# A convolution and a Mamba layer on one core: decays made two units ahead, and TensorE in order of emission in the last image

## The chip, the cores and the metric

The kernel runs on one core of a Trainium2 chip, as one program and one launch. A core has a TensorE (PE: matrix multiplications and transposes, into PSUM), a VectorE (DVE), a ScalarE (ACT), a GpSimd (POOL) and a SyncE (SP, which issues most of the transfers here). Each engine works through its own list of instructions in order, and waits at semaphores for the others. The metric is the time of one execution in microseconds (us) on the device. Times are medians of several executions; the profile is one more execution, recorded by the hardware profiler.

## The reference

The input x holds four images of 128 x 128 positions and 128 channels, float32. Two layers follow each other, each adding to x:

```python
x = x + _L0_conv_ref(_gn(x), ...)   # deformable 3x3 convolution, two groups of 64 channels
x = x + _L1_conv_ref(_gn(x), ...)   # two Mamba blocks along each row
```

`_gn` normalises groups of four channels over a whole image. The first layer predicts nine offsets for each position and group by a 3x3 convolution, samples the image bilinearly there, and multiplies with a depthwise and a pointwise weight. The second layer treats each row of an image as a sequence of 128 steps. One of its two Mamba blocks is:

```python
u, res = split(h @ in_w)                       # 128 -> 2 x 256
u = silu(conv1d(u) + cb)                       # causal, 4 taps, per channel
dt, Bm, Cm = split(u @ xw)                     # 8, 16, 16
delta = softplus(dt @ dtw + dtb)
h_t = exp(delta_t * A) * h_(t-1) + delta_t * u_t * Bm_t     # 256 channels x 16 states
y_t = sum over the states of h_t * Cm_t, plus u_t * Dp
out = (y * silu(res)) @ ow
```

So each row needs a scan over 128 steps for 256 x 16 channel and state pairs: a decay exp(delta A), an input delta u B, the scan, the product with C and the sum over the states.

## The kernel before

**Stages.** The normalisation of the second layer needs the whole image after the first, so image b of the second layer runs beside image b+1 of the first. The program has: the first layer of image 0 alone (to about 3.3 ms); three mixed stages (second layer of image 0, 1, 2 beside the first layer of image 1, 2, 3); and the second layer of the last image alone (from about 20.12 ms).

**First layer.** For each four rows and each of nine taps POOL gathers the corner pixels with indirect DMAs (`gather`, L370), DVE or ACT multiplies them with the bilinear weights (`sample`, `gw`, L398 on DVE and L393 on ACT, 16 instructions of 64 columns there), PE transposes and sums them (`p`, L137), ACT copies them out (`s`, L416, L417, L413), and PE multiplies with the weights (`acc`, L427). These names turn up in the mixed stages beside the second layer's.

**Second layer.** A job is one block of four rows (512 columns) and one of the two Mamba blocks; an image has 64 jobs, in pairs of blocks, so that a job's successor does not depend on it. `pre` makes what the scan needs, in pieces between which the job before it goes on: the projection with the convolution's four taps (`pu`, L554), SiLU (`u`, L564), the gate (`pr`, L569; `g`, L574), B, C and dt (`pdb`, L578; `dbl`, L581; B and C go to DRAM as `bcd`), and softplus. Softplus is made of Abs and Relu of `pdt` (L600, L603, L604), Exp (L605), 1 + e (L606), Ln (L607) and one step that takes back the rounding of 1 + e. In the first three images PE adds up the four terms by multiplying with the identity (`pdl`, L621, copied out at L622); in the last image DVE does it in three operations (L611 to L613). Then `du` = delta u (L624).

`main` runs the scan in eight units of two states each. For one unit:
- ACT makes the decays into a buffer `da` [128, 2 channel halves, 2 states, 4 rows, 128 steps]: a zero for the first step of each row (L655), and four Exp (L660). There are three such buffers (`das`, `NDA = 3`).
- In the first three images B and C come from DRAM spread over the partitions (`bc0`, `bc1`, issued on SP); DVE multiplies `du` with B (`hs`, L694), scans 2048 columns at once (L700), and multiplies with C (L703). In the last image POOL and ACT multiply the transposed `du` (`duts`, made in `turn_du`) with B (`xs`, L679 for the first state on POOL, L677 for the second on ACT), PE transposes it back (`px`, L684, 16 transposes into four PSUM banks, of which there are four), DVE scans four times 512 columns (L686) and multiplies with C (L689).
- PE transposes the result and adds it to `y` in PSUM (L137, `y`, 16 instructions a unit). There is one `y`, which the job starts with u D (L639).

After the eighth unit comes the job's tail: `g` = y gate on DVE (L710), its transposes (`pyg`, L715), copies (`yg`, L716), the output projection (`pout`, L720, or L727 and L729 with the residual), and a copy out (L722, L733).

**What sets the order.** The Python program emits all instructions in one sequence: `layer1` goes through the jobs, advances `pre` of the next job by one piece after each unit (`next(nxt, None)`), and the loop at the end puts steps of the first layer between the units. The compiler of the framework then schedules: on each engine it takes, by its own model of the costs, the earliest emitted instruction that is ready. The list that results is fixed; on the chip an engine waits at its next instruction, whatever stands behind it. A tile pool with a given number of buffers lets a new tile in when an old one is released. With `manual_schedule` an engine's instructions keep the order of emission.

Of the kernel before, what the change touches and what calls it, by code (L numbers as in the profile page):

```python
# [10 lines left out]
F32 = mybir.dt.float32  # L11
I32 = mybir.dt.int32
AF = mybir.ActivationFunctionType
ALU = mybir.AluOpType
# [3 lines left out]
P = 128  # L18
# [4 lines left out]
SR = 4  # L23
TB = SR * P
# [3 lines left out]
NC = 2  # L28
NS = 16
NQ = 2  # L30
# [34 lines left out]
def block_kernel(ctx: ExitStack, tc: tile.TileContext, a: dict, out: bass.AP):  # L65
# [69 lines left out]
    def add_transposed(o, v, start, stop):  # L135

        nc.tensor.matmul(o, v, ident, is_transpose=True, start=start, stop=stop, skip_group_check=True)  # L137
# [342 lines left out]
    NDA = 3  # L480
# [32 lines left out]
    def in_last(blk):  # L513

        return blk * SR // H == B - 1
# [19 lines left out]
    def pre(st, l):  # L535
# [68 lines left out]
            nc.scalar.activation(de[:, c], pdt, AF.Relu)  # L604
        nc.scalar.activation(e, e, AF.Exp, scale=-1.0)  # L605
        nc.scalar.activation(w1, e, AF.Identity, bias=1.0)  # L606
        nc.scalar.activation(du, w1, AF.Ln)  # L607
        if in_last(blk):
            nc.scalar.activation(w1, w1, AF.Identity, bias=-1.0)
            yield  # L610
            nc.vector.tensor_tensor(e, w1, e, ALU.subtract)  # L611
            nc.vector.tensor_tensor(de, de, e, ALU.subtract)
            nc.vector.tensor_tensor(de, de, du, ALU.add)  # L613
        else:
            nc.scalar.activation(w1, w1, AF.Identity, scale=-1.0, bias=1.0)
            yield
            yield
            for c in range(NC):
                pdl = now["ps1"].tile([P, TB], F32, tag="t", name=f"pdl_{nm}_{c}")
                for k, v in enumerate((e, w1, du, de)):  # L620
                    nc.tensor.matmul(pdl, ident, v[:, c], start=(k == 0), stop=(k == 3))  # L621
                nc.scalar.copy(de[:, c], pdl)  # L622
# [5 lines left out]
            yield  # L628
            turn_du(st, nm)

    def main(st, l):
# [11 lines left out]
        if in_last(blk) and "dut" not in st:  # L643
            turn_du(st, nm)
        for q in range(NS // NQ):
            bc = []
            for w in range(in_last(blk), 2):
                t = lm[0].tile([P, NQ, TB], F32, tag=f"bc{w}", name=f"bc{w}_{nm}_{q}", bufs=2)
                n0 = w * NS + q * NQ
                nc.sync.dma_start(t, st["bcd"][n0 : n0 + NQ, :].partition_broadcast(P))  # L650
                bc.append(t)
            da = das[n_da[0] % NDA]
            n_da[0] += 1

            nc.scalar.copy(da.rearrange("p c n s t -> p (c n s) t")[:, :, 0], zero)  # L655
            for c in range(NC):
                dv = st["delta"][:, c].rearrange("p (s t) -> p s t", s=SR)
                for n in range(NQ):
                    s = q * NQ + n
                    nc.scalar.activation(  # L660
                        da[:, c, n, :, 1:], dv[:, :, 1:], AF.Exp, scale=aneg[:, l, c, s : s + 1]
                    )
            dc = da.rearrange("p c n s t -> p c (n s t)")
            cv = bc[-1].rearrange("p n t -> p (n t)").unsqueeze(1).to_broadcast([P, NC, NQ * TB])
            if in_last(blk):


                for n in range(NQ):
                    s = q * NQ + n

                    xs = lm[0].tile(
                        [P, SR, NC * P], F32, tag="bc0" if n else "gw", name=f"xs_{nm}_{s}", bufs=2
                    )
                    for i in range(SR):
                        bv = st["bt"][:, i, s : s + 1]
                        if n:
                            nc.scalar.activation(xs[:, i], st["dut"][:, i], AF.Copy, scale=bv)  # L677
                        else:
                            nc.gpsimd.tensor_scalar(xs[:, i], st["dut"][:, i], bv, None, ALU.mult)  # L679
                    for c in range(NC):  # L680
                        pool, tag = (now["ps"], "t") if n else (psa, "acc")
                        px = pool.tile([P, SR, P], F32, tag=tag, name=f"px_{nm}_{s}_{c}")
                        for i in range(SR):
                            nc.tensor.transpose(px[:, i, :], xs[:, i, c * P : (c + 1) * P], ident)  # L684
                        dn = da[:, c, n].rearrange("p s t -> p (s t)")
                        nc.vector.tensor_tensor_scan(  # L686
                            dn, dn, px.rearrange("p s t -> p (s t)"), 0.0, ALU.mult, ALU.add
                        )
                nc.vector.tensor_tensor(dc, dc, cv, ALU.mult)  # L689
            else:  # L690
                hs = lm[0].tile([P, NC, NQ, TB], F32, tag="hs", name=f"hs_{nm}_{q}")

                for n in range(NQ):
                    nc.vector.scalar_tensor_tensor(  # L694
                        hs[:, :, n, :], st["du"], one,
                        bc[0][:, n].unsqueeze(1).to_broadcast([P, NC, TB]),
                        op0=ALU.mult, op1=ALU.mult,
                    )
                df = da.rearrange("p c n s t -> p (c n s t)")
                nc.vector.tensor_tensor_scan(  # L700
                    df, df, hs.rearrange("p c n t -> p (c n t)"), 0.0, ALU.mult, ALU.add
                )
                nc.vector.scalar_tensor_tensor(dc, dc, one, cv, op0=ALU.mult, op1=ALU.mult)  # L703
            for c in range(NC):
                for n in range(NQ):
                    for i in range(SR):
                        add_transposed(y[:, i, c], da[:, c, n, i, :], False, q == NS // NQ - 1 and n == NQ - 1)
            yield
        gt = st["g"]
        nc.vector.tensor_tensor(gt, y.rearrange("p s c d -> p s (c d)"), gt, ALU.mult)  # L710
        yg = lm[0].tile([P, NC, TB], F32, tag="yg", name=f"yg_{nm}")
        for c in range(NC):
            pt = now["ps1"].tile([P, SR, P], F32, tag="t", name=f"pyg_{nm}_{c}")
            for i in range(SR):
                nc.tensor.transpose(pt[:, i, :], gt[:, i, c * P : (c + 1) * P], ident)  # L715
            nc.scalar.copy(yg[:, c], pt.rearrange("p s t -> p (s t)"))  # L716
        po = now["ps1"].tile([P, TB], F32, tag="t", name=f"pout_{nm}")
        if l < NL - 1:
            for c in range(NC):
                nc.tensor.matmul(po, ow[:, l, c, :], yg[:, c], start=(c == 0), stop=(c == NC - 1))  # L720
# [136 lines left out]
```

## Time and profile before

| what | value |
|---|---|
| median of 3 executions | 24469.56 us (24467.03 to 24477.43) |
| profiled execution, its own time | 24467.72 us |
| its span in the profile | 24465.9 us, 304806 instructions |
| scans of the mixed stages on DVE (L700) | 1536, 4.42 us each, 3357.9 to 20123.5 us |
| scans of the last image (L686) | 2048, 1.20 us each, 20148.8 to 24448.4 us |
| decays on ACT (L660) | 8192, 0.71 us each |
| DVE busy | 20647.2 us (84% of the span) |
| the profile's granted PE clock, mean | 0.928 |

How to read the profile. An instruction is named by engine, line of the kernel, operation, what it writes and what it reads. A row of a timeline gives its start, its duration, and in brackets the idle time of the engine ahead of it and what ended it; `x16` at the end means 16 instructions one after another. A group's or line's row gives min, median and max of one in ns, and below it in us and times what its engine sat idle for ahead of it. A row of windows gives start and end, its length, then the busy time of PE, PE's weight loads (PEld), DVE, ACT and POOL with the number of instructions, the granted PE clock, the DMA share and GB/s. A row of waits gives who waited, for whom, us in total, times, and the longest. PE's matmul in float32 shows as two instructions.

### The profile page before, as it was taken

The numbers are of one execution on the slowest core, as the hardware profiler recorded it, in microseconds if no ns is written. First come the engines' busy times: TensorE is split into PE (matmuls) and PEld (weight loads), VectorE is DVE, ScalarE is ACT, GpSimd is POOL, SyncE is SP. The second block draws the span as 40 slices with busy tenths as digits, with TensorE's granted clock in tenths as the row PEclk, the third lists the DMA queues.
The fourth block names the chain that finished last, engine by engine and source line by source line (L and its number), as shares of the span: only waits on it lengthen the run. The fifth ranks groups of instructions, "written<-read, shape, count | busy, mean of one in ns | idle before, by whom it ended". The sixth has DMA issues, their size and how long they took to land. (4 is left out here: it accounts for less than half of the span.)

```text
span 24465.9 us, 304806 instructions
## 1 busy us (share of the span) xinstructions
PE 20571.8 (84%) x109348; PEld 12814.4 (52%) x109348; DVE 20647.2 (84%) x12769; ACT 15875.8 (65%) x36074; POOL 18054.1 (74%) x11270
## 2 busy tenths in 40 slices
PE   5777788888888888888888888888988878777777
PEld 3444445555555555555555555555555546666666
DVE  3332369999999999999999999999999998888888
ACT  1111147777777767777777766777777768888887
POOL 4777778888888857888888857888888845555555
PEclk7888889999999999999999999999999989999999
DMA  5554544554545544554555544455545532222221
GB/s 150 155 157 125 149 132 160 162 162 163 163 161 165 162 148 161 162 162 162 162 164 163 163 148 159 163 161 163 164 162 164 162 126 69 70 70 70 69 70 68
DMA packets 1530702, 3470.14 MB, mean 142 GB/s; under 512 B 243283, under 2 KB 717651, under 8 KB 1529052
## 3 DMA queue, kind: packets, MB, share of 16 engines
q1 hardware_dynamic: 1086812, 2242.08, 28.5%
q0 software_dynamic: 442368, 1208.55, 15.5%
q8 instruction: 859, 14.07, 0.2%
q14 instruction: 663, 5.43, 0.1%
HBM read 3299.19 MB, written 150.47 MB: 141 GB/s over the span
## 5 line engine op out<-in xcount | busy, mean ns | idle before, releaser
L370 POOL DMA_INDIRECT gt<-table,idx x9216 | 15702.9, 1704 | 4130.4 <-issue 2793.6
L700 DVE TENSOR_TENSOR_SCAN da<-da,hs 128x2048 f32<-128x2048 f32 x1536 | 6792.7, 4422 | 810.7 <-ACT da L660 708.2
L660 ACT ACTIVATE da<-de,aneg 128x508 f32<-128x508 f32 x8192 | 5450.1, 711 | 1447.6 <-PE y L137 1313.8
L427 PE MATMUL acc<-s,wc 128*64 128x512 f32 (+2 forms) x23520 | 5854.9, 609 | 143.0 <-ACT s L416 136.1
L137 PE MATMUL y<-ident,da 128*128 128x128 f32 x32768 | 4410.3, 291 | 1187.1 <-DVE da L703 911.6
L137 PEld LDWEIGHTS y<-ident,da 128*128 128x128 f32 x32768 | 3936.2, 150 | 2099.3 <-DVE da L703 1028.3
L679 POOL TENSOR_SCALAR xs<-duts,bt 128x256 f32<-128x256 f32 x2048 | 2350.4, 1164 | 2249.6 <-ACT duts L532 1190.4
L694 DVE SCALAR_TENSOR_TENSOR hs<-du,misc,bc 128x1024 f32<-128x1024 f32 x3072 | 3829.4, 1283 | 0.2
L137 PE MATMUL p<-ident,gw 128*128 128x128 f32 x18432 | 2592.6, 293 | 1375.2 <-DVE gw L398 1359.0
L427 PEld LDWEIGHTS acc<-s,wc 128*64 128x64 f32 (+1 forms) x23520 | 1940.7, 141 | 3368.5 <-issue 2999.7
L703 DVE SCALAR_TENSOR_TENSOR da<-da,misc,bc 128x2048 f32<-128x2048 f32 x1536 | 3609.3, 2350 | 39.0
L398 DVE TENSOR_TENSOR gw<-gt,wt 128x1024 f32<-128x1024 f32 x1440 | 1756.1, 1220 | 2219.3 <-DMA gt<-table,idx 2010.2
L393 ACT ACTIVATE gw<-gt,wt 128x64 f32<-128x64 f32 x13824 | 3487.9, 337 | 93.0 <-DMA gt<-table,idx 86.0
L137 PEld LDWEIGHTS p<-ident,gw 128*128 128x128 f32 x18432 | 2247.6, 151 | 1972.1 <-DVE gw L398 1513.7
L686 DVE TENSOR_TENSOR_SCAN da<-da,px 128x512 f32<-128x512 f32 x2048 | 2350.4, 1202 | 506.6 <-PE px L684 506.6
L416 ACT COPY s<-p 128x512 f32<-128x512 f32 x1152 | 671.3, 583 | 2332.7 <-PE p L137 2330.6
L554 PE MATMUL pu<-hp,inc 128*128 128x512 f32 x4096 | 1823.0, 593 | 0.2 <-ACT duts L532 0.2
L684 PE MATMUL px<-ident,xs 128*128 128x128 f32 x8192 | 1210.6, 287 | 542.9 <-DVE da L686 328.2
L684 PEld LDWEIGHTS px<-ident,xs 128*128 128x128 f32 x8192 | 968.5, 147 | 824.1 <-POOL xs L679 331.0
L413 ACT COPY s<-halo 128x256 f32<-128x256 f32 x1116 | 433.4, 401 | 1220.4 <-PE acc L427 1218.4
L689 DVE TENSOR_TENSOR da<-da,bc 128x2048 f32<-128x2048 f32 x512 | 1172.2, 2290 | 6.5
L554 PEld LDWEIGHTS pu<-hp,inc 128*128 128x128 f32 x4096 | 746.9, 189 | 821.1 <-issue 820.4
(148 smaller groups left out, 17815.0 us busy)
## 6 DMA issues: line engine op xcount, KB each, us to landing
bc<-bcd SPq DMA_DIRECT2D x3584, 512.0 KB
gt<-table,idx POOLq DMA_INDIRECT x9216
table<-xg SPq DMA_DIRECT2D x1016, 64.0 KB
xt<-in_x SPq DMA_DIRECT2D x124, 320.0 KB
xr<-in_x SPq DMA_DIRECT2D x128, 256.0 KB
x<-xo SPq DMA_DIRECT2D x128, 256.0 KB
x1t<-x SPq DMA_DIRECT2D x128, 256.0 KB
x1t_o<-x SPq DMA_DIRECT2D x128, 256.0 KB
```

The source lines that it names most:

```text
L137: nc.tensor.matmul(o, v, ident, is_transpose=True, start=start, stop=stop, skip_group_check=True)
L370: nc.gpsimd.indirect_dma_start(out=gt[:, v, r], out_offset=None, in_=flat, in_offset=bass.IndirectOffsetOnAxis(ap=idx[:, ri, o : o + 1], a ...
L393: nc.scalar.activation(gw[:, r, s, v], gts[h][:, v, r, s * CG : (s + 1) * CG], AF.Copy, scale=wt[:, u, r0 + r, s, v : v + 1],)
L427: nc.tensor.matmul(accs[b, j][CG * g : CG * g + CG, q, :], wc[sl, v, e, :], st[p + 4 * g if p < 4 else 8][sl, ky + q.start : ky + q.stop, ...
L554: nc.tensor.matmul(px.rearrange("p (s t) -> p s t", s=SR), inc[:, l, j, c * P : (c + 1) * P], h[:, :, j : j + P], start=(j == 0), stop=(j ...
L660: nc.scalar.activation(da[:, c, n, :, 1:], dv[:, :, 1:], AF.Exp, scale=aneg[:, l, c, s : s + 1])
L679: nc.gpsimd.tensor_scalar(xs[:, i], st["dut"][:, i], bv, None, ALU.mult)
L684: nc.tensor.transpose(px[:, i, :], xs[:, i, c * P : (c + 1) * P], ident)
L686: nc.vector.tensor_tensor_scan(dn, dn, px.rearrange("p s t -> p (s t)"), 0.0, ALU.mult, ALU.add)
L694: nc.vector.scalar_tensor_tensor(hs[:, :, n, :], st["du"], one, bc[0][:, n].unsqueeze(1).to_broadcast([P, NC, TB]), op0=ALU.mult, op1=ALU. ...
L700: nc.vector.tensor_tensor_scan(df, df, hs.rearrange("p c n t -> p (c n t)"), 0.0, ALU.mult, ALU.add)
L703: nc.vector.scalar_tensor_tensor(dc, dc, one, cv, op0=ALU.mult, op1=ALU.mult)
```

## The change

Four things are changed.

1. The decays become a function of their own, `decays`. Two units are made ahead at the start, and then each unit emits the decays of the unit two later, directly after its product with C, ahead of its own transposes. A queue runs over all jobs, so the decays of a job's first two units are emitted in units 6 and 7 of the job before. `delta` is handed over as soon as it is made.
2. What else a unit needs, the broadcasts of B and C and in the last image `xs` and `px`, becomes `head`, and is emitted one unit ahead, before the transposes of `y`; the first unit of a job has its `head` in the last unit of the job before (`after`, which first finishes `pre`). The job's tail is emitted ahead of the step of the first layer, no longer behind it.
3. In the last image PE keeps the order of emission (`manual_schedule`).
4. In the last image softplus is added up by PE as in the others, and the three DVE operations go. In the other images there is one more break between the pieces of `pre`, ahead of Ln.

```diff
         nc.scalar.activation(w1, e, AF.Identity, bias=1.0)
+        if not in_last(blk):
+            yield
         nc.scalar.activation(du, w1, AF.Ln)
-        if in_last(blk):
-            nc.scalar.activation(w1, w1, AF.Identity, bias=-1.0)
+        nc.scalar.activation(w1, w1, AF.Identity, scale=-1.0, bias=1.0)
+        yield
+        if not in_last(blk):
             yield
-            nc.vector.tensor_tensor(e, w1, e, ALU.subtract)
-            nc.vector.tensor_tensor(de, de, e, ALU.subtract)
-            nc.vector.tensor_tensor(de, de, du, ALU.add)
-        else:
...
+        for c in range(NC):
+            pdl = now["ps1"].tile([P, TB], F32, tag="t", name=f"pdl_{nm}_{c}")
+            for k, v in enumerate((e, w1, du, de)):
+                nc.tensor.matmul(pdl, ident, v[:, c], start=(k == 0), stop=(k == 3))
+            nc.scalar.copy(de[:, c], pdl)
+        st["delta"] = de
+        if not in_last(blk):
             yield
         nc.vector.tensor_tensor(du, de, u, ALU.mult)
...
+    def decays(st, l, q):
+        da = das[n_da[0] % NDA]
+        n_da[0] += 1
+        nc.scalar.copy(da.rearrange("p c n s t -> p (c n s) t")[:, :, 0], zero)
...
+                nc.scalar.activation(
+                    da[:, c, n, :, 1:], dv[:, :, 1:], AF.Exp, scale=aneg[:, l, c, s : s + 1]
+                )
+        made.append(da)
+    def head(st, l, q):
...
+        if in_last(blk) and "dut" not in st:
+            turn_du(st, nm)
...
+            nc.sync.dma_start(t, st["bcd"][n0 : n0 + NQ, :].partition_broadcast(P))
...
+                for c in range(NC):
+                    pool, tag = (now["ps"], "t") if n else (psa, "acc")
+                    px = pool.tile([P, SR, P], F32, tag=tag, name=f"px_{nm}_{s}_{c}")
+                    for i in range(SR):
+                        nc.tensor.transpose(px[:, i, :], xs[:, i, c * P : (c + 1) * P], ident)
+                    pxs[n, c] = px
+        return bc, pxs
+    def main(st, l, first, after):
...
+        ahead = first
         for q in range(NS // NQ):
+            bc, pxs = ahead
+            da = made.pop(0)
...
+            last = q == NS // NQ - 1
+            for f in queue[:1]:
+                decays(*queue.pop(0))
+            ahead = after() if last else head(st, l, q + 1)
             for c in range(NC):
                 for n in range(NQ):
                     for i in range(SR):
...
-            yield
+            if not last:
+                yield
...
+    queue = [(st, l, q) for st, l in jobs for q in range(NS // NQ)]
+    made = []
     def layer1():
...
+        for _ in range(NDA - 1):
+            decays(*queue.pop(0))
+        firsts = {0: head(*jobs[0], 0)}
         for i, job in enumerate(jobs):
+            if i and in_last(job[0]["blk"]) and not in_last(jobs[i - 1][0]["blk"]):
+                ctx.enter_context(tc.manual_schedule(engines={mybir.EngineType.PE}))
             nxt = pre(*jobs[i + 1]) if i + 1 < len(jobs) else iter(())
+            def after(i=i, nxt=nxt):
+                for _ in nxt:
+                    pass
+                if i + 1 < len(jobs):
+                    firsts[i + 1] = head(*jobs[i + 1], 0)
-            for _ in main(*job):
+            for _ in main(*job, firsts.pop(i), after):
                 next(nxt, None)
                 yield
-            for _ in nxt:
-                pass
+            yield
```

More of the change, by code (lines that the diff above doesn't have):

```diff
@@ L606, in pre @@
         nc.scalar.activation(w1, e, AF.Identity, bias=1.0)
+        if not in_last(blk):
+            yield
         nc.scalar.activation(du, w1, AF.Ln)
-        if in_last(blk):
-            nc.scalar.activation(w1, w1, AF.Identity, bias=-1.0)
+        nc.scalar.activation(w1, w1, AF.Identity, scale=-1.0, bias=1.0)
+        yield
+        if not in_last(blk):
             yield
-            nc.vector.tensor_tensor(e, w1, e, ALU.subtract)
-            nc.vector.tensor_tensor(de, de, e, ALU.subtract)
-            nc.vector.tensor_tensor(de, de, du, ALU.add)
-        else:
-            nc.scalar.activation(w1, w1, AF.Identity, scale=-1.0, bias=1.0)
-            yield
[L617 to L622, printed above, removed]
+        for c in range(NC):
[5 more added lines that the diff above has]
+        if not in_last(blk):
             yield
@@ L629, in pre @@
             turn_du(st, nm)
-    def main(st, l):
+    def decays(st, l, q):
[3 more added lines that the diff above has]
+        for c in range(NC):
+            dv = st["delta"][:, c].rearrange("p (s t) -> p s t", s=SR)
+            for n in range(NQ):
+                s = q * NQ + n
+                nc.scalar.activation(
[3 more added lines that the diff above has]
+    def head(st, l, q):
+        blk = st["blk"]
+        nm = f"{blk}_{l}"
+        if in_last(blk) and "dut" not in st:
+            turn_du(st, nm)
+        bc = []
+        for w in range(in_last(blk), 2):
+            t = lm[0].tile([P, NQ, TB], F32, tag=f"bc{w}", name=f"bc{w}_{nm}_{q}", bufs=2)
+            n0 = w * NS + q * NQ
+            nc.sync.dma_start(t, st["bcd"][n0 : n0 + NQ, :].partition_broadcast(P))
+            bc.append(t)
+        pxs = {}
+        if in_last(blk):
+            for n in range(NQ):
+                s = q * NQ + n
+                xs = lm[0].tile(
+                    [P, SR, NC * P], F32, tag="bc0" if n else "gw", name=f"xs_{nm}_{s}", bufs=2
+                )
+                for i in range(SR):
+                    bv = st["bt"][:, i, s : s + 1]
+                    if n:
+                        nc.scalar.activation(xs[:, i], st["dut"][:, i], AF.Copy, scale=bv)
+                    else:
+                        nc.gpsimd.tensor_scalar(xs[:, i], st["dut"][:, i], bv, None, ALU.mult)
+                for c in range(NC):
+                    pool, tag = (now["ps"], "t") if n else (psa, "acc")
+                    px = pool.tile([P, SR, P], F32, tag=tag, name=f"px_{nm}_{s}_{c}")
+                    for i in range(SR):
+                        nc.tensor.transpose(px[:, i, :], xs[:, i, c * P : (c + 1) * P], ident)
+                    pxs[n, c] = px
+        return bc, pxs
+    def main(st, l, first, after):
         blk = st["blk"]
@@ L642, in main @@
                 )
-        if in_last(blk) and "dut" not in st:
-            turn_du(st, nm)
+        ahead = first
         for q in range(NS // NQ):
[L646 to L662, printed above, removed]
+            bc, pxs = ahead
+            da = made.pop(0)
             dc = da.rearrange("p c n s t -> p c (n s t)")
@@ L668, in main @@
                 for n in range(NQ):
[L669 to L679, printed above, removed]
                     for c in range(NC):
[L681 to L684, printed above, removed]
                         dn = da[:, c, n].rearrange("p s t -> p (s t)")
                         nc.vector.tensor_tensor_scan(
-                            dn, dn, px.rearrange("p s t -> p (s t)"), 0.0, ALU.mult, ALU.add
+                            dn, dn, pxs[n, c].rearrange("p s t -> p (s t)"), 0.0, ALU.mult, ALU.add
                         )
@@ L706, in main @@
                     for i in range(SR):
-                        add_transposed(y[:, i, c], da[:, c, n, i, :], False, q == NS // NQ - 1 and n == NQ - 1)
-            yield
+                        add_transposed(y[:, i, c], da[:, c, n, i, :], False, last and n == NQ - 1)
+            if not last:
+                yield
         gt = st["g"]
```

## The prediction

> **What bounds the kernel now.** I read the windows by stage first, then what VectorE (DVE) waits for, then the timelines at the waits.
>
> ```profile
> PE 20571.8 (84%) x109348; PEld 12814.4 (52%) x109348; DVE 20647.2 (84%) x12769; ACT 15875.8 (65%) x36074; POOL 18054.1 (74%) x11270
> 3700.00:9150.00 5450.00, 4774.61 (x24640) 2854.55 (x24640) 5109.80 (x2740) 3874.45 (x9388) 4364.02 (x2258) 0.94 0.50 161
> ...
> 20125.00:24460.00 4335.00, 3462.46 (x21631) 2697.95 (x21632) 3810.94 (x2879) 3471.50 (x6213) 2350.45 (x2048) 0.94 0.21 69
> ```
>
> The columns are PE, PEld, DVE, ACT, POOL. In the three mixed stages (second line) DVE is busy 94%, in the last image 88%. So DVE bounds both, and what counts is its idle time.
>
> ```profile
> L700 DVE TENSOR_TENSOR_SCAN da<-da,hs x1536: 4351/4425/4491, 3357.9 to 20123.5; 128x2048 f32<-128x2048 f32 x192
>   ACT da L660: 708.2, 152
> ...
> DVE da L686 <- PE px L684: 506.6, 145, 13.4
> ```
>
> DVE's idle time has two causes. In the mixed stages the scan waits 708.2 us for decays from ScalarE (ACT). In the last image it waits 506.6 us for TensorE's (PE's) transposes. One wait of the first kind:
>
> ```profile
> 7797.29 0.71 ACT L660 ACTIVATE da<-de,aneg 128x508 f32<-128x508 f32 x1
> ...
> 7803.46 1.06 ACT L605 ACTIVATE e<-e 128x1024 f32<-128x1024 f32 x1
> ...
> 7807.26 1.06 ACT L607 ACTIVATE du<-w 128x1024 f32<-128x1024 f32 x1
> ...
> 7810.57 1.28 ACT L660 ACT_TABLE_LOAD   x1
> ...
> 7814.48 0.71 ACT L660 ACTIVATE da<-de,aneg 128x508 f32<-128x508 f32 x1
> 7815.22 4.42 DVE L700 TENSOR_TENSOR_SCAN da<-da,hs 128x2048 f32<-128x2048 f32 x1 [6.02 <-ACT da L660]
> ```
>
> Between one unit's last decay (7797.29) and the next unit's (7814.48) ACT has done the next job's softplus, 16 sampling products and two table loads: 17.2 us, where DVE needs about 10.4 us a unit (jobs start 87.4 us apart there; less 3.7 us of waits, over 8). I numbered the units in their jobs: 682 of the 708 us belong to scans with such a block in front of their last decay.
>
> And the last image, DVE first, then PE:
>
> ```profile
> 21038.38 2.26 DVE L689 TENSOR_TENSOR da<-da,bc 128x2048 f32<-128x2048 f32 x1
> 21047.30 3.44 DVE L686 TENSOR_TENSOR_SCAN da<-da,px 128x512 f32<-128x512 f32 x3 [6.66 <-PE px L684]
> ...
> 21037.98 3.60 PE L554 MATMUL pu<-hp,inc 128*128 128x512 f32 x8
> 21041.42 1.91 PE L137 MATMUL y<-ident,da 128*128 128x128 f32 x16
> 21043.16 3.60 PE L554 MATMUL pu<-hp,inc 128*128 128x512 f32 x8
> 21046.60 1.47 PE L684 MATMUL px<-ident,xs 128*128 128x128 f32 x12
> ```
>
> PE does the next job's projection before the transposes that DVE waits for. Such waits are 530 us in 64 jobs, 8.3 of a job's 67.5 us. The other 59.2 us DVE works.
>
> **The change, part by part.** Where each instruction of the changed kernel stands on its engine is read from the program's lists; durations are from the rows of before.
>
> *Mixed stages, decays two units ahead.* Of ACT's order I counted, in each of some 190 jobs, in front of which unit's last decay the softplus's Ln stands, and summed ACT's work from the last decay before it. Before: unit 4 in 21 jobs (22.1 us of work), unit 5 in 64 (18.0), unit 6 in 104 (15.4). The waits at those units are 186, 308 and 188 us, so 8.9, 4.8 and 1.8 a job: in each case about the block less 13.3 us (22.1 - 8.9, 18.0 - 4.8, 15.4 - 1.8). After: unit 6 in 189 jobs, mean 11.3 us; 34 blocks are near 16 us, the rest 12 or less. By the same rule 34 x 2.7 = 92 us are left, and 590 of 682 go. ACT's total work and the table loads of these stages stay (793 loads before, 775 after). What DVE then runs into: a decay's buffer is free only after PE's transposes of three units earlier (ACT waited 997 us for those between 4000 and 20000), and PE falls behind at each job's start, because y has one buffer (around 7760, unit 0's product ends on DVE at 7759.6 and its transposes start at 7774.37, behind the job before's tail); POOL is busy 80%, and 0.3 us lie between two of its gathers. Softplus moves a unit later, so du stands directly ahead of its first scan, where before a unit lay between. I give 70 us for all this: -520 us. Bounds: 0 (the block, now always at unit 6, costs the time it saved at 4 and 5) and -682.
>
> SP's broadcasts move ahead of the transposes; no scan waited for one, and none is added. The output's tail goes ahead of the image's sampling step: same instructions, nothing on DVE.
>
> *Last image, softplus on PE.* Three DVE operations a job go (L611 to L613, 1.13 us each in a row): -3.4 us. PE gains 16 matmul instructions, 8 pairs at 0.86 us:
>
> ```profile
> 8164.48 1.02 PE L621 MATMUL pdl<-e,ident 128*128 128x512 f32 x2
> ...
> 8170.68 1.02 PE L621 MATMUL pdl<-de,ident 128*128 128x512 f32 x2
> ```
>
> That is 6.9 us; ACT gains two copies (0.48 each) and, by its order, 8 table loads a job instead of 6: 3.5 us on 54.2 of 67.5, hidden by its idle time.
>
> *Last image, PE in order of emission.* The order of a unit q is: px(q+1), y(q), then a piece of the next job. I walked one job, from the end of unit 4 on DVE, with a DVE unit of 6.75 us (4 x 1.13 + 2.2), px 1.85, y 1.8:
> - The projection pieces: the rest of px 1.4, y 1.8, the piece 3.45 and the next first px 0.5 make 7.15 us against DVE's 6.75: it waits 0.4 twice. This replaces the wait of 6.66 shown.
> - After y(5) comes the sum pdl. It needs the last softplus step on ACT. ACT gets pdt 2.8 us after unit 4 ends, needs 8.6 (21063.52 to 21072.1 in the timeline) and now also stands waiting for y(5) with a buffer's first column ahead of Ln: ready at 12.4, when PE, there at 8.65, has waited 2.9 us. pdl ends at 18.5, px(7) is there at 19.1, DVE was ready at 13.5: 5.6 us of waiting. Queued behind pdl are px(7), y(6) and pdu.
> - Then du, pdu and two copies; POOL multiplies xs (0.92 to 1.17 us each, five ahead of the fourth needed) and the next job's first px is there 3.0 us late (from du's end, 21.3 on the walk's clock, to 29.8; DVE was ready at 26.9). y(7) stands behind it on PE.
> - The tail: g, pyg, copies, pout (21030.49 to 21035.06 in the timeline for g's start to pout's end, 4.6 us; about 1 more in the second layer), all of the next y's start (1.9) and px (0.6) now stand in front of the second unit's scans: 4.6 + 0.5 + 1.9 + 0.6 less g's own 1.1 on DVE, 6.4 us.
>
> Waits 0.8 + 5.6 + 3.0 + 6.4 = 15.8 instead of 8.3. A job is 59.2 - 3.4 + 15.8 = 71.6 us, 4.1 more, x 64 = +260 us. Bounds: if ACT and POOL are never late, 2.4 for pdl, 1.8 for POOL (five at 0.92), 5.5 for the tail and 0.4 leave 65.9 us, -100; if each of the three hand-overs through ACT meets one more table load (1.3), +500. I take the walk, whose rows are of this stage.
>
> **Two rules of the Trainium skill.** In the rows a table load takes 1283 ns and the next activation starts 10 ns later (21068.49 and 21069.78). "ScalarE: Activation LUTs", What ACT_TABLE_LOAD costs, gives 2.66 us with a drain, which would make pdl's wait 1.4 us longer, +90 us; no such drain is in these rows, so I leave it out.
> PE is busy 80% of the last image and PEld 62%. "Perfetto Trace Analysis", Identifying the Most-Contended Engine, counts PE's room by LDWEIGHTS: by it 6.9 us more would fit, and the sum would be the second rival's. The walk says otherwise, because of PE's order and not of its load.
>
> **The sum.** -520 + 260 = -260 on the profiled execution's 24467.7 (span 24465.9 and 1.8 around it): 24208. The median shown is 1.9 above it: 24210.
>
> **Rivals.**
> - *Slower.* PE's late y holds ACT at the decays, which now stand ahead of softplus, and what queues behind them (softplus, sampling products, copies) comes as late as before: only 120 of the 590 us go. It speaks for it that PE's y is what ACT waits for most; against it that the waits sit at the softplus blocks. 24467.7 - 120 + 260 = 24608. It decides once less than 260 us go, that is once more than 2.3 of the 3.7 us that a job waits now (708 us in 192 jobs) stay.
> - *Both gain.* The order of emission does what it looks like, px is there before each scan, waits of some 3.5 us a job remain: 59.2 - 3.4 + 3.5 = 59.3, -525 us in the last image: 24467.7 - 520 - 525 = 23420. Against it: the three in-order waits walked above.
> - *No change.* The waits move from units 4 and 5 to unit 6 (104 jobs there waited 1.8 each; 189 x 1.8 = 340 left, 340 saved) and the last image costs 340 too, inside its bounds: 24468.
>
> **How the numbers follow.** Forecast 0.52, own range 23990 to 24420 (main -650 to -350, last +130 to +350); slower 0.23; both gain 0.13; no change 0.12. The range 23850 to 24640 leaves out most of the second rival and the far end of the first. A measurement tells 0.2% (49 us) from no change. Faster: 0.51 + 0.13 + 0.03 = 0.67; same: 0.01 + 0.02 + 0.07 = 0.10; slower 0.23.
>
> **What would show it.** In the profile after: the scan's wait for decays under 150 us and at unit 6 alone (right), or above 450 (first rival); a DVE mixed stage busy 97% and about 170 us shorter; a last image 4.55 to 4.65 ms long, DVE waiting for px at units 1, 7 and 0 of each job, with pdl ahead of px on PE. Wrong if softplus on ACT comes earlier against PE than walked, or if gathers become what DVE waits for.

## The result, and the profile after

The changed kernel takes 24690.4 us (median of 4 runs, 24678.8 to 24706.8) against 24473.5 us of the kernel before on the same chip: a ratio of 1.0088, 95% interval 1.0072 to 1.0104. It is slower by 217 us, where 260 us less were forecast. The profiled execution has a span of 24686.8 us.

First the page's line of busy times of the changed kernel, then two windows, one in the first mixed stage and one over the last image (columns: stretch, its length, busy time of PE, PEld, DVE, ACT and POOL, granted clock, DMA share, GB/s).

```profile
PE 21088.9 (85%) x110372; PEld 13054.0 (53%) x110372; DVE 20500.3 (83%) x12577; ACT 16067.7 (65%) x36312; POOL 17978.0 (73%) x11270
3700.00:8800.00 5100.00, 4586.69 (x23801) 2716.89 (x23800) 4903.09 (x2628) 3726.28 (x9062) 4260.32 (x2191) 0.95 0.51 165
19778.00:24669.00 4891.00, 3992.29 (x22562) 2989.01 (x22563) 3624.76 (x2682) 3678.51 (x6447) 2144.15 (x2037) 0.89 0.18 61
```

In the mixed stage DVE is now busy 96% (4903.09 of 5100) instead of 94%. In the last image it is busy 74% instead of 88%, and the clock that PE was granted there has fallen from 0.94 to 0.89. From DVE's first product with C to its last (L705) the last image takes 4891 us instead of 4296: 595 us more. From the first scan of the mixed stages to the last image's first product it is 3370.9 to 19778.0 instead of 3357.9 to 20153.4: 388 us less. These two make the result; the 13 us by which the first scan starts later are the rest of it, but for a few us.

What DVE's scan in the mixed stages waited for, and then DVE's longest wait in the last image:

```profile
L716 DVE TENSOR_TENSOR_SCAN da<-da,hs x1536: 4352/4425/4493, 3370.9 to 19760.6; 128x2048 f32<-128x2048 f32 x192
  ACT da L639: 199.2, 102
  PE y L137: 28.7, 10
...
DVE da L702 <- PE px L676: 1247.7, 210, 9.7
```

The wait for decays fell from 708.2 to 199.2 us. The wait for px rose from 506.6 to 1247.7 us.

One job of the last image, DVE from unit 6's product on (L705 is the product, L702 the scan, L622 du, L731 the gate), then PE over the same time:

```profile
21361.56 2.29 DVE L705 TENSOR_TENSOR da<-da,bc 128x2048 f32<-128x2048 f32 x1
21371.94 1.22 DVE L702 TENSOR_TENSOR_SCAN da<-da,px 128x512 f32<-128x512 f32 x1 [8.09 <-PE px L676]
21373.08 1.20 DVE L622 TENSOR_TENSOR du<-de,u 128x1024 f32<-128x1024 f32 x1
...
21383.11 4.55 DVE L702 TENSOR_TENSOR_SCAN da<-da,px 128x512 f32<-128x512 f32 x4 [3.16 <-PE px L676]
21387.70 2.29 DVE L705 TENSOR_TENSOR da<-da,bc 128x2048 f32<-128x2048 f32 x1
21389.91 1.22 DVE L731 TENSOR_TENSOR g<-y,g 128x1024 f32<-128x1024 f32 x1
21399.48 4.55 DVE L702 TENSOR_TENSOR_SCAN da<-da,px 128x512 f32<-128x512 f32 x4 [8.36 <-PE px L676]
...
21359.28 1.02 PE L617 MATMUL pdl<-e,ident 128*128 128x512 f32 x2
21363.56 2.08 PE L617 MATMUL pdl<-w,ident 128*128 128x512 f32 x2 [3.25 <-ACT w L610]
21365.42 1.68 PE L617 MATMUL pdl<-du,ident 128*128 128x512 f32 x2
21366.94 1.02 PE L617 MATMUL pdl<-de,ident 128*128 128x512 f32 x2
...
21371.23 1.91 PE L676 MATMUL px<-ident,xs 128*128 128x128 f32 x16
...
21391.18 1.97 PE L736 MATMUL pyg<-ident,g 128*128 128x128 f32 x8 [2.96 <-DVE g L731]
21392.97 3.78 PE L741 MATMUL pout<-yg,w_ow 128*128 128x512 f32 x4
21396.54 2.39 PE L688 MATMUL y<-ddiag,u 128*128 128x128 f32 x16
21398.78 1.91 PE L676 MATMUL px<-ident,xs 128*128 128x128 f32 x16
```

The three waits stand where the prediction put them: behind pdl at unit 7 (8.09), behind POOL's xs at unit 0 of the next job (3.16) and behind the tail at its unit 1 (8.36). Over all jobs they average 8.4, 3.2 and 7.6 us. What was not foreseen is seen in PE's durations: the pair of w behind the wait takes 2.08 us and the same pair without a wait 1.02; pout takes 3.78 us. The windows over this job show why (last but two column: granted clock; the fourth and fifth are cut where the clock changes):

```profile
21362.00:21366.00 4.00, 2.44 (x3) 1.18 (x4) 1.85 (x1) 2.30 (x5) 0.00 (x0) 0.67 0.27 81
21370.00:21374.00 4.00, 4.00 (x30) 3.23 (x29) 2.06 (x2) 3.52 (x6) 0.00 (x0) 1.00 0.00 0
21382.00:21386.00 4.00, 3.58 (x17) 3.40 (x17) 2.89 (x3) 0.00 (x0) 4.00 (x5) 0.50 0.17 64
21387.23:21390.63 3.40, 0.99 (x9) 0.75 (x7) 3.37 (x3) 3.11 (x8) 3.40 (x2) 1.00 0.00 0
21390.64:21397.47 6.83, 6.29 (x17) 4.00 (x18) 0.49 (x1) 2.40 (x5) 0.14 (x1) 0.50 0.20 77
21398.00:21402.00 4.00, 4.00 (x39) 4.00 (x38) 2.52 (x3) 1.22 (x3) 2.02 (x3) 1.00 0.03 6
```

After each wait of about 3 us PE runs at half speed for some us, and in the last of these stretches (clock 0.50 from 21390.64 to 21397.47) it does so while everything on the path behind it (pyg, pout, the next y's start) is waited for. PE's last product ahead of it had ended at 21388.2, so the clock was halved 2.4 us into the wait. "TensorE: Matmul & The Clock Gate" in the Trainium skill, Part 1 (The HAM clock gate), says that PE's clock is halved once PE has idled for a window of about 3.4 us, and is given back after about as long a busy one. The trace agrees on the half (0.50 in two windows, 2.08 against 1.02 us); that the clock fell 2.4 us into a wait of 2.96 us is below the page's figure.

### The profile page after: what moved, and what is told of

The parts are those of the page before. It is cut to its first block, busy times and chain, and to the rows that moved or that the text cites. A ratio compares the mean times of both kernels' runs of the same rounds, so it can differ in the third digit from the quotient of the medians.

```text
span 24686.8 us, 306803 instructions
## 1 busy us (share of the span) xinstructions
PE 21088.9 (85%) x110372; PEld 13054.0 (53%) x110372; DVE 20500.3 (83%) x12577; ACT 16067.7 (65%) x36312; POOL 17978.0 (73%) x11270
## 4 chain that ended last, share of the span: by engine, by line
POOL 24%; PE 24%; DVE 16%; issue 16%; ACT 14%; DMA 5%; SPq 0%; DVEq 0%; POOLq 0%; ACTq 0%
POOL gt L370 23%; DVE da L716 6%; ACT da L639 5%; PE acc L427 5%; DMA gt<-table,idx 4%; PE pdl L617 4%; DVE hs L710 3%; PE pu L554 3%; PE y L137 3%; DVE da L719 3%; PE px L676 2%; POOL xs L671 1%; ACT gw L393 1%; DVE da L702 1%; PE y L688 1%
## 5 line engine op out<-in xcount | busy, mean ns | idle before, releaser
L716 DVE TENSOR_TENSOR_SCAN da<-da,hs 128x2048 f32<-128x2048 f32 x1536 | 6791.7, 4422 | 339.1 <-ACT da L639 199.2
L137 PE MATMUL y<-ident,da 128*128 128x128 f32 x32768 | 4316.5, 284 | 530.7 <-DVE da L719 466.8
L137 PEld LDWEIGHTS y<-ident,da 128*128 128x128 f32 x32768 | 3856.3, 147 | 1239.7 <-DVE da L719 578.0
L671 POOL TENSOR_SCALAR xs<-duts,bt 128x256 f32<-128x256 f32 x2048 | 2156.4, 1072 | 2993.4 <-ACT duts L532 1712.9
L137 PE MATMUL p<-ident,gw 128*128 128x128 f32 x18432 | 2724.8, 291 | 1292.7 <-DVE gw L398 1153.2
L702 DVE TENSOR_TENSOR_SCAN da<-da,px 128x512 f32<-128x512 f32 x2048 | 2336.6, 1201 | 1253.9 <-PE px L676 1247.7
L705 DVE TENSOR_TENSOR da<-da,bc 128x2048 f32<-128x2048 f32 x512 | 1173.5, 2292 | 17.3
L736 PE MATMUL pyg<-ident,g 128*128 128x128 f32 x2048 | 424.6, 375 | 840.5 <-DVE g L731 840.4
```

The lines of the kernel that those rows point to most:

```text
L702: nc.vector.tensor_tensor_scan(dn, dn, pxs[n, c].rearrange("p s t -> p (s t)"), 0.0, ALU.mult, ALU.add)
L716: nc.vector.tensor_tensor_scan(df, df, hs.rearrange("p c n t -> p (c n t)"), 0.0, ALU.mult, ALU.add)
```

## The experiments

The theories were: M, the order of emission on PE makes the last image slow; S, the softplus on PE does; C, PE's slow clock after its waits enlarges what M makes. After the first three runs two more came up: H, the heads and decays ahead cost in the last image; and within H, D (decays) against P (heads). The table has, of each profiled run, the ratio of its time to that of the kernel before measured beside it, and from the last image the stretch from first to last product, the mean job and the granted clock.

| kernel | ratio, 95% | last image, us | job, us | clock |
|---|---|---|---|---|
| before | 1 | 4296 | 67.4 | 0.94 |
| changed | 1.0088 (1.0072 to 1.0104) | 4891 | 76.7 | 0.89 |
| ahead_only | 0.9955 (0.9938 to 0.9971) | 4564 | 71.7 | 0.85 |
| dve_soft | 1.0065 (1.0049 to 1.0082) | 4836 | 75.9 | 0.82 |
| pe_sched | 0.9985 (0.9975 to 0.9994) | 4650 | 73.0 | 0.89 |
| mix_only | 0.9842 (0.9826 to 0.9859) | 4309 | 67.6 | 0.93 |
| mix_dec | 0.9886 (0.9870 to 0.9903) | 4382 | 68.8 | 0.92 |
| mix_head | 0.9941 (0.9924 to 0.9957) | 4527 | 71.1 | 0.86 |
| mix_soft | 0.9903 (0.9887 to 0.9920) | 4426 | 69.5 | 0.95 |
| px_first | 1.0122 (1.0106 to 1.0139) | 4986 | 78.2 | 0.88 |
| tail_late | 1.0040 (1.0026 to 1.0054) | 4779 | 75.1 | 0.89 |
| filler | 1.0045 (1.0028 to 1.0062) | 4809 | 75.4 | 0.92 |
| warm | 1.0068 (1.0051 to 1.0085) | 4840 | 75.9 | 0.96 |
| warm2 | 1.0051 (1.0034 to 1.0068) | 4782 | 75.0 | 0.95 |

Beside mix_dec, mix_head, mix_soft and warm the kernel before itself took 25,022 us, and beside warm2 25,068 us, and the first scan of the kernels tried came at about 3900 us instead of 3360; these are compared by their ratios and by their last image.

**The changed kernel taken apart: ahead_only, dve_soft, pe_sched.**

```
dve_soft:    softplus of the last image as in the kernel before
             (w1 - 1; e = w1 - e; de = de - e; de = de + du on VectorE)
pe_sched:  - ctx.enter_context(tc.manual_schedule(engines={mybir.EngineType.PE}))
ahead_only:  both
```

> Only the decays two units ahead (with the heads opened early) are kept; in the last image TensorE is ordered by the planner again and VectorE sums the softplus, as in the kernel before. Both theories expect the 388 us of the stages of two images and no loss behind them: about 24,085 us (24,020 to 24,150), with 4.25 to 4.35 ms between the last image's first and last product. If the decays ahead were themselves part of the last image's loss, it lies above 24,200.

> The changed kernel with VectorE summing the softplus in the last image; TensorE's order of emission is kept. If that order is what costs (theory M), the waits for px at units 0 and 1 stay and the one at unit 7 goes, while VectorE gets 3.4 us a job more: the last image stays at 4.55 to 4.9 ms, total 24,350 to 24,700. If the softplus on TensorE is what costs (rival S), the last image returns to about 4.3 ms, total 24,050 to 24,150.

> The changed kernel with the last image's TensorE ordered by the planner; TensorE still sums the softplus there. If the order of emission costs (theory M), the job falls from 76.8 us to 64 to 67 us, the last image to 4.1 to 4.25 ms, total 23,900 to 24,050. If the softplus on TensorE costs (rival S: 6.9 us more of TensorE a job and two more table loads on ScalarE), the job stays above 72 us, the last image above 4.6 ms, total above 24,400.

They took 24360.8, 24634.0 and 24437.6 us beside 24472.4 of the kernel before. With the run of the changed kernel these are the four corners of a square. The order of emission costs 272 us of last image without the softplus (4564 to 4836) and 241 with it (4650 to 4891). The softplus on PE costs 86 without the order (4564 to 4650) and 55 with it (4836 to 4891). So M is the larger of the two. But both theories had 24,085 us for ahead_only, and it missed that by 276 us: with neither the order nor the softplus the last image takes 4564 us instead of 4296. DVE waits there 364.6 us for px and 313.3 us for decays, the latter at unit 0 of the next job, where the scans' order puts it (the expectation of mix_dec below has unit 6). The expectation for pe_sched, a job of 64 to 67 us, failed for the same reason: with the order back at the compiler's planner the job still takes 73.0 us, so the order of emission is not the whole cause. In dve_soft the wait at unit 7 is gone, and yet the job is only 0.9 us shorter: 3 operations came back to DVE, and the wait at unit 0 rose from 3.2 to 7.4 us.

**The gain alone: mix_only.**

```
-            for f in queue[:1]:
+            for f in [] if in_last(blk) else queue[:1]:
                 decays(*queue.pop(0))
-            ahead = after() if last else head(st, l, q + 1)
+            if not in_last(blk):
+                ahead = after() if last else head(st, l, q + 1)
+            else:
+                ahead = None
...
```

In the last image the decays, xs and px stand at their own unit, and the rest of the preparation comes after the tail; the planner's order and the softplus on DVE are back as in ahead_only.

> The decays two units ahead and the early heads only where two images are mixed; the last image is as in the kernel before (decays at their own unit, planner's order, softplus on VectorE). The run with the decays and heads ahead everywhere took 24,361 us, with 71.7 us a job in the last image against 67.4 before. If decays and heads ahead cost there (theory H), this one has 67 to 68 us a job and a total of 24,050 to 24,130 us, the whole gain of the mixed stages. If the last image is slow because of the state that the mixed stages leave (rival), it stays above 70 us a job and 24,300 us.

It took 24082.4 us beside 24464.2: 382 us less. The window of its last image, and DVE's two waits over the whole execution:

```profile
19797.00:24106.00 4309.00, 3471.41 (x21544) 2709.74 (x21544) 3796.30 (x2871) 3461.54 (x6194) 2343.94 (x2036) 0.93 0.20 70
...
DVE da L712 <- PE px L684: 507.2, 139, 8.3
DVE da L726 <- ACT da L645: 211.4, 98, 6.0
```

DVE waits for px 507.2 us, as in the kernel before (506.6), and for decays 211.4 us (L726 is the scan of the mixed stages), near the 199.2 of the changed kernel. The last image is what it was but for 13 us, and by the medians the gain of the mixed stages is nearly whole. In the profiled execution, which took 42 us more than the median, they gain 358 us and not 388. The rival, a state left by the mixed stages, is out. This version beats both kernels.

**Decays or heads: mix_dec and mix_head.** Each adds one thing to mix_only in the last image: the decays two units ahead, or the next unit's head ahead of this unit's y (and with it, at the last unit, the rest of the next job's preparation ahead of the tail).

```
mix_dec:   -            for f in [] if in_last(blk) else queue[:1]:
           +            for f in queue[:1]:
mix_head:  +            ahead = after() if last else head(st, l, q + 1)
           ...
```

> The kernel with the new order in the mixed stages alone (24,082 us, 67.6 us a job in the last image) plus one thing: in the last image the decays are emitted two units ahead too; px and xs stay at their own unit. With both ahead the job takes 71.7 us, and the scan of unit 6 waits 4.9 us for decays. If the decays two ahead cost this (theory D: their third buffer waits for y of the unit just done), the job lies at 70 to 72 us, total 24,240 to 24,380. If the heads do (theory P), it stays at 67 to 68.5 us, total 24,050 to 24,140.

> The same base plus the other thing: in the last image the next unit's xs and px are emitted ahead of this unit's y (and the rest of the next job's preparation ahead of the tail); the decays stay at their own unit. Theory P: 70 to 72 us a job, total 24,240 to 24,380, and the granted clock of TensorE in the last image falls from 0.93 towards 0.85. Theory D: 67 to 68.5 us, total 24,050 to 24,140.

The decays alone lengthen the last image by 73 us (4382 against 4309), the heads alone by 218 (4527). Their sum, 291, is near what both cost together (255, ahead_only against mix_only). The waits are not the same, though: the 313.3 us for decays of ahead_only are in neither (mix_dec 0, mix_head 0), they come with both ahead. So theory P is the larger part and D a small one; D's own job of 70 to 72 us did not come (68.8).

```profile
20357.00:24884.00 4527.00, 3501.83 (x21543) 2762.78 (x21542) 3826.28 (x2870) 3587.49 (x6317) 2200.28 (x2036) 0.86 0.20 66
...
DVE da L712 <- PE px L684: 680.3, 128, 6.2
```

With the heads ahead DVE waits 178 us more for px than in mix_only (680.3 against 502.2 of the last image): 5.9 us a job at unit 0, where mix_only waits 0.5, and 4.8 instead of 7.3 at unit 2. DVE's work is 30 us more. The wait of the kernel before became smaller, as the change intends, and a larger one came at unit 0. PE's clock is 0.86 there; whether that or the order counts for more was not told apart.

**The softplus alone: mix_soft.** mix_only with TensorE summing the softplus in the last image, as in the changed kernel.

> The same base plus TensorE summing the softplus in the last image. By the two pairs measured so far this sum costs 56 to 77 us: total 24,130 to 24,170. If it was dear only because px already stood ahead of y, and the planner's order of before hides it, VectorE's 3.4 us a job come back in part: 23,900 to 24,080.

The last image takes 117 us more (4426 against 4309) at a clock of 0.95. The hope that the planner hides it failed: DVE is busy 199 us less and waits for px 795.5 us, 293 more, of which 4.4 us a job are a new wait at unit 6. With the two pairs above the softplus on PE costs 55 to 117 us in each of three surroundings.

**Another order: px_first and tail_late.**

```
px_first:   +            if not last and in_last(blk):
            +                yield          # ahead of this unit's y
tail_late:   px_first, and in the last image the gate, pyg, pout and the next
             y's start are emitted after the px of the next job's unit 1
```

> The changed kernel; in the last image a piece of the next job's preparation is emitted between the next unit's px and this unit's y, so that it no longer waits on TensorE behind y. If the order among these three is what makes px late (theory M), px at unit 7 comes earlier by up to the 3.9 us of y and the wait there falls from 8.4 to 4 to 6 us a job; the job falls by 1 to 4 us: total 24,430 to 24,630. If only the wait for the preparation's own inputs counts, the total stays at 24,650 to 24,750.

> As the run with the preparation between px and y, and in the last image the job's tail (gate, pyg, pout, the next y's start) is emitted after the px of the next job's unit 1. If the tail ahead of px is what makes unit 1 wait (theory M: 7.6 us a job), that wait goes and comes back as no other: 64 to 70 us a job, total 24,000 to 24,300. If the wait only moves (to unit 2, whose decays need the y that the tail holds up, or to px at unit 0), the job stays above 73 us, total above 24,450.

px_first is slower still: 95 us more in the last image. The wait for px at unit 7 went (8.4 to 0.3 us), as theory M said, and others took its place: du now waits 576.5 us for delta's copy, 9.2 in each of 63 jobs, and the scans 85.2 us for decays. In tail_late the wait at unit 1 went too (7.6 to nothing), and 5.0 us came at unit 2. One job of tail_late (L622 is du):

```profile
21381.72 2.29 DVE L709 TENSOR_TENSOR da<-da,bc 128x2048 f32<-128x2048 f32 x1
21392.61 1.22 DVE L622 TENSOR_TENSOR du<-de,u 128x1024 f32<-128x1024 f32 x1 [8.60 <-ACT de L618]
21394.18 4.55 DVE L706 TENSOR_TENSOR_SCAN da<-da,px 128x512 f32<-128x512 f32 x4 [0.34 <-PE px L676]
```

DVE executes in its own order too: du stands ahead of unit 7's scan there, and what du waits for (the sum pdl and its copy) is as late as before: 546.1 us in 63 jobs, 8.7 each. In the changed kernel du stood behind one scan that waited as long. So 8 us a job at the end of the job hang on the chain w, pdl, copy, du, and not on which transposes stand beside it. Against px_first, from which it differs by the place of the tail alone, tail_late's last image is 207 us shorter; against the changed kernel it is 112. Its job of 75.1 us misses the 64 to 70 us that were expected by 5.

**The clock: filler, warm, warm2.** Extra products of TensorE, each overwritten by what follows, fill its waits.

```
filler:   +  for _ in range(5 if in_last(blk) and c == 0 else 0):
          +      nc.tensor.matmul(pdl, ident, e[:, 0], start=True, stop=True)
warm:     filler; 10 transposes of ident ahead of each of four parts of a job's
          first px; 20 ahead of pyg
warm2:    filler; 40 transposes of ident ahead of pyg
```

> The changed kernel; in the last image five extra products of e go to TensorE ahead of each job's first sum of the softplus, where it stands idle for 3.2 us; each is overwritten by the sum itself, so the result does not change. If TensorE runs slowly because it had idled (theory C), the products of w and du behind the wait return from 2.08 and 1.68 us a pair to about 1.0, the granted clock in the last image rises above 0.89, and the job falls by 1 to 2.5 us: total 24,530 to 24,630. If the idle time does not matter, these pairs stay at about 2 us and the total at 24,660 to 24,750.

> The changed kernel with TensorE kept busy in the last image: the five extra products ahead of the softplus's sum as before, ten extra transposes of the identity ahead of each of the four parts of a job's first px (it waits there for GpSimd), and twenty ahead of pyg (it waits there for the gate). If the slow clock after these waits is the other part of the loss (theory C), pyg and pout return from 1.97 and 3.78 us to about 1.1 and 1.9, the granted clock rises to 0.97 or more, and the job falls below that of the run with the first filling alone (75.4 us) by 2 to 4.5 us: total 24,290 to 24,450. If the waits themselves are the loss, or the filling delays what it precedes, the total stays at 24,550 or above.

> The run with TensorE kept busy left 2.87 us of idle time ahead of pyg, and pyg, pout and the next y's start stayed at 1.97, 3.78 and 2.39 us. This one has the five extra products ahead of the softplus's sum and forty transposes of the identity ahead of pyg (about 4.5 us, nearly all of the wait there), none ahead of px. If the slow clock behind that wait is part of the loss at unit 1 (theory C), pyg, pout and start return to about 1.1, 1.9 and 1.9 us, the wait at unit 1 falls from 7.5 to 4 to 6 us, and the ratio to the kernel before falls from the 1.0045 of the first filling to 0.995 to 1.000. If the order alone makes that wait, the ratio stays at 1.004 to 1.008.

filler behaves as theory C says: its ratio is 1.0045 against 1.0088, the last image is 82 us shorter, and the pairs are back:

```profile
21422.16 4.46 PE L617 MATMUL pdl<-e,ident 128*128 128x512 f32 x10
21426.45 1.02 PE L619 MATMUL pdl<-e,ident 128*128 128x512 f32 x2
21427.31 1.02 PE L619 MATMUL pdl<-w,ident 128*128 128x512 f32 x2
21428.17 1.02 PE L619 MATMUL pdl<-du,ident 128*128 128x512 f32 x2
```

PE was busy 119 us more there (4110.95 against 3992.29) and the kernel became faster: here idle time on an engine was dearer than useless work. The wait at unit 7 went from 8.4 to 7.3 us.

warm did not answer its question. Its twenty transposes ahead of pyg were done too early, 2.87 us of idle time stayed, and pyg, pout and the start were as slow as before; ten transposes ahead of each part of px held px up a little (3.4 instead of 3.2 us). warm2 filled that wait:

```profile
21948.97 4.53 PE L739 MATMUL pyg<-ident 128*128 128x128 f32 x40
21953.34 1.04 PE L741 MATMUL pyg<-ident,g 128*128 128x128 f32 x8
21954.61 1.98 PE L746 MATMUL pout<-yg,w_ow 128*128 128x512 f32 x4 [0.24 <-ACT yg L742]
21956.43 1.95 PE L690 MATMUL y<-ddiag,u 128*128 128x128 f32 x16
...
21951.00 1.22 DVE L733 TENSOR_TENSOR g<-y,g 128x1024 f32<-128x1024 f32 x1
21958.92 4.55 DVE L704 TENSOR_TENSOR_SCAN da<-da,px 128x512 f32<-128x512 f32 x4 [6.71 <-PE px L678]
```

pyg, pout and start returned to 1.04, 1.98 and 1.95 us, as theory C said. The wait at unit 1 hardly moved over all jobs (7.4 instead of 7.5 us), and the ratio (1.0051) is not below that of filler. The rows show the reason: the forty transposes ended at 21953.5, 1.3 us after the gate (21952.2), so they held up pyg by what the faster clock brought. Over the 64 jobs the mean from pyg's start to the scan is 7.5 us in filler and 6.1 in warm2, while pyg starts 1.4 us after the gate instead of 0.05. So the slow clock costs 1.4 us of the 7.5 at unit 1, and this filling took as much; that a filling without this delay would gain it was not shown by a time.

**Without a result: mix_pu and mix_nb.** Two more versions of mix_only were to show whether the wait at unit 2 goes when each pu of the last image comes one unit later (mix_pu), and what the extra break ahead of Ln gives in the mixed stages (mix_nb). Neither gave a time, so both questions stay open.

## Why the prediction was wrong

**Mixed stages, -520: measured -388; the mechanism was right, the size too large.** The rule (the block of ACT's work less 13.3 us) left 92 of 682 us of waits; 199.2 of 708.2 are left. So 509 us went instead of 590. They are not at unit 6 alone: unit 4 has 112 us in 31 jobs, unit 5 has 72 and unit 6 has 45 (with some of other releasers). For the 27 longest at unit 4 the trace has 200 us of ACT's idle time in the 22 us before the scan, 91 of it just ahead of the Silu of pu: there ACT waits for PE's projection, and the rule knows only ACT's own work. That this idle time is what the scans wait for was not tested. The 70 us for what DVE would run into instead became 121: DVE's waits for y (28.7), the offsets' loc (30 more), du (30 more) and the gathers (21 more) sum to 110 of them. mix_only shows that this part stands by itself, 382 us. A stage was to be 170 us shorter with DVE at 97%; from first scan to first scan the three are 142, 112 and 135 us shorter (5462 instead of 5604 in the first) at 96%. What the extra break ahead of Ln gives of it stays open.

**Last image, +260: measured +595. This step failed.** Its three waits were found in the places named, so the walk was right in its mechanism, and its terms were mis-sized:
- pdl at unit 7: 5.6 predicted, 8.4 measured. In the job shown PE gets w 0.3 us before DVE is free (21363.56 against 21363.85) where the walk had 1.1, which is 0.8 us; and the pairs of w and du cost 2.08 + 1.68 instead of 1.02 each, 1.7 us more. filler shows that the second part is the clock. Every price in the walk was taken from rows in which PE had not idled, and the walk itself made PE idle.
- The tail at unit 1: 6.4 predicted, 7.6 measured, with pyg, pout and the start at 1.97, 3.78 and 2.39 us in the job shown instead of 1.1, 1.9 and 1.9. By warm2 the slow clock is 1.4 us of it, about what was missed.
- POOL's xs at unit 0: 3.0 predicted, 3.2 measured. The pieces of the projection: 0.8 predicted, 0.3 measured.
- DVE's own work: 55.8 predicted. 3624.76 us in 4891 / 76.75 = 63.7 jobs are 56.9. Of the 1.1 missed, 0.4 is the walk's start: it took waits of 8.3 and so 59.2 of work, where the profile has 506.6 us of waits, 7.9 a job, and 59.6 of work (3797 us in 63.7 jobs). The rest is that the work fell by 2.7 us a job and not 3.4.
So waits of 19.5 us instead of 15.8, and work of 56.9 instead of 55.8: 4.8 us a job, 306 us of the 335 missed.

By the edits, the order of emission is 241 to 272 us of the 595, the heads ahead about 220, the decays ahead about 70 and the softplus 55 to 117. The prediction priced the head's place only as a part of the order of emission. ahead_only shows that it costs with the planner as well, and that was seen by no step of the prediction.

**The rivals.** "Slower" had the sign and nearly the time (24608), but by another mechanism: it kept the waits for decays in the mixed stages, and those went. "Both gain" is refuted in its second half; its first half is mix_only. "No change" is refuted: the waits did not move to unit 6. Of the two rules weighed, the one on room by weight loads would have had the softplus fit on PE; mix_soft, at a clock of 0.95, says that it does not. The table loads are as the rows had them: in the last image of ahead_only they still take 1283 ns each.

**Open:** how far the slow clock, apart from the order, makes the loss of the heads ahead (mix_head, 0.86); whether the 1.4 us a job of slow clock at unit 1 can be won back; and whether the wait at unit 2 that the kernel before has (7.2 us a job, some 460 us) can go without another in its place.

## What to carry to other kernels

Take a change apart by stage before judging it: this one holds a gain of 388 us and a loss of 595 us, and the version with the gain alone (mix_only) is 1.6% faster than the kernel before. When a walk in order of emission makes an engine wait, its rows from a busy stretch no longer hold for what follows the wait; here PE's work behind an idle stretch of 3 us took up to twice as long. And when transposes are put first in a queue that other engines feed, look for the chain that then stands last (here w, pdl, copy, du): moving its neighbours only moves the wait.

## What the runs showed of the hardware that was not expected

PE's granted clock follows its own idle time within a job: 1.00, then 0.50 for 6.8 us (21390.64 to 21397.47) from 2.4 us into a wait of 3 us on, then 1.00 again. Useless products in such a wait made the kernel faster (ratio 1.0045 against 1.0088). And the same 21,544 or so products in the last image took 3471 us at a clock of 0.93 (mix_only) and 3721 us at 0.82 (dve_soft).
